# A memset on GpSimd behind every indirect gather of a deformable convolution

## The chip, the core and the metric

The kernel runs on one core of a Trainium2 chip. The metric is device microseconds (us) for one execution of the whole program; a kernel's time is the median over several runs. A profiled execution is a separate run with the hardware profiler on, and it is longer than the plain ones, so both are given below.

## The reference, cut to what matters

Eight images of 256 channels and 64x64 pixels go through two layers. Each layer group-normalises its input and adds its result to it. Layer 0 is a 3x3 neighbourhood attention with four heads. Layer 1 is a modulated deformable 3x3 convolution: an ordinary 3x3 convolution predicts, for every pixel and each of nine taps, a place to read at and a weight; the four corners round that place are fetched, weighted and summed, and the result is multiplied with the weights of that tap.

```python
x = x + _L0_conv_ref(_gn(x), ...)          # attention
om = conv3x3(_gn(x), w_off) + b_off        # 27 numbers a pixel
py, px = base + tap + om[:18]              # where each of 9 taps reads
v = samp(y0, x0) * ((1 - ly) * (1 - lx)) + samp(y0, x0 + 1) * ((1 - ly) * lx) \
  + samp(y0 + 1, x0) * (ly * (1 - lx)) + samp(y0 + 1, x0 + 1) * (ly * lx)
v = v * sigmoid(om[18:27])
x = x + einsum('bckhw,ock->bohw', v, w)
```

`samp` reads all 256 channels of one pixel, wherever the offset points. That is what the gathers of this case do.

## The kernel before

Work is cut by image (8), by chunk of 8 image rows (8 to an image, 512 pixels each), by tap (9 to a chunk) and by block of 128 pixels (4 to a tap). An image therefore has 72 taps and 288 blocks (`SLOTS`, `BLOCKS`), and the program has 2,304 blocks.

Two streams of work are written out by hand and interleaved under a manual schedule, so each engine runs its instructions in the order in which the code issues them.

The front stream (`fronts`, line 752) does for one image the attention (`attention`, line 555) and then the preparation of layer 1 (`prepare`, line 624): it writes the normalised pixels as rows into a table in DRAM (`to_table`, line 630; each row holds two vertically adjacent pixels, `ts` goes out by SyncE at line 645), predicts the offsets (`offsets`, line 649) and turns them into row indices and corner weights (`positions`, line 668). It also loads the next image (line 91) and takes its statistics on VectorE (line 261).

The sampling stream works on the image before. For each block there are four steps, each in its own function:

- `gather` (line 765): GpSimd issues one indirect DMA (line 771). It fetches for 128 pixels the four corners, 4 KB a pixel, from the table into a buffer `g` of 128 x 1,024 floats. There are ten such buffers (`GATHERS`).
- `scale` (line 779): ScalarE multiplies corner 0 into a sum `s` (line 787).
- `sum_corners` (line 790): VectorE adds corners 1 to 3 with three instructions a block (line 795), two blocks at a time. After the third, the buffer `g` is free.
- `transposes` and `product` (lines 809 and 822): TensorE turns the four sums of a tap (line 816), ScalarE copies them out of PSUM (`vt`, line 819), and TensorE multiplies them with that tap's weights into `po` (line 833). After nine taps `finished` (line 841) adds the residual on VectorE (line 844) and SyncE stores the chunk.

`ahead(i)` (line 799) fixes how far each step runs before the tap that uses it, and the order in which the engines' queues are filled:

```python
scale(i + SCALE_AHEAD)        # 8 blocks ahead, two blocks
scale(i + SCALE_AHEAD + 1)
sum_corners(i + SUM_AHEAD)    # 6 blocks ahead, two blocks
gather(i + LEAD)              # 18 blocks ahead, two blocks
gather(i + LEAD + 1)
```

It is called twice a tap, with a piece of the front stream issued between (line 891). The gather of block i+18 takes the buffer of block i+8. So it waits until VectorE has summed block i+8, which is issued one call of `ahead` later; GpSimd, whose queue holds nothing but gathers after the start, stands at its next gather until a buffer comes free. The last image has no front stream beside it: its 72 taps run alone.

Of the kernel before, what the change touches and what calls it, by code (L numbers as in the profile page):

```python
# [9 lines left out]
F32 = mybir.dt.float32  # L10
# [7 lines left out]
P = 128  # L18
# [30 lines left out]
SUM_AHEAD = 6  # L49
SCALE_AHEAD = SUM_AHEAD + 2  # L50
GATHERS = 10
LEAD = SCALE_AHEAD + GATHERS
STEPS = 2 + 7 * NC + 6 + NC + 1
STEPS_AHEAD = 6
# [3 lines left out]
def preact_kernel(ctx: ExitStack, tc: tile.TileContext, a: dict, out: bass.AP):  # L58
# [17 lines left out]
    nc = tc.nc  # L76
    x = a["x"]
    B = x.shape[0]

    const = ctx.enter_context(tc.tile_pool(name="const", bufs=1))  # L80
# [15 lines left out]
    def const_tile(name, shape):  # L96
        t = const.tile(shape, F32, tag=name, name=name)
        nc.scalar.dma_start(t, a[name])
        return t


    alpha = const_tile("alpha", [P, 1])
    gp = ctx.enter_context(tc.tile_pool(name="gp", bufs=GATHERS))
    w_qkv = [gp.tile([96, 4, C], F32, tag="g", name=f"w_qkv{i}") for i in range(2)]
# [38 lines left out]
    with (  # L143
# [26 lines left out]
        for i in range(min(2, B)):  # L170
# [3 lines left out]
            for o in range(H * WP, ENTRIES, P):  # L174
                n = min(P, ENTRIES - o)
# [585 lines left out]

    rows: dict = {}
    sums: dict = {}

    def gather(i):
        if i >= B * BLOCKS:
            return
        b, n = divmod(i, BLOCKS)
        c, k, j = n // NB // KK, n // NB % KK, n % NB
        g = gp.tile([P, 4 * C], F32, tag="g", name=f"g_{i}")  # L770
        nc.gpsimd.indirect_dma_start(  # L771
            out=g,
            out_offset=None,
            in_=tables[b % 2],
            in_offset=bass.IndirectOffsetOnAxis(ap=found[b, c][0][:, j, k : k + 1], axis=1),
        )
        rows[i] = g

    def scale(i):

        if i >= B * BLOCKS:
            return
        b, n = divmod(i, BLOCKS)
        c, k, j = n // NB // KK, n // NB % KK, n % NB
        s = gp.tile([P, C], F32, tag="s", name=f"s_{i}", bufs=NB + SUM_AHEAD)
        g, w = rows.pop(i), found[b, c][1][:, j, k]
        nc.scalar.activation(s, g[:, 0:C], AF.Copy, scale=w[:, 0:1])  # L787
        sums[i] = s, g, w

    def sum_corners(i):  # L790

        work = [sums[n] for n in (i, i + 1) if n in sums]
        for q in range(1, 4):
            for s, g, w in work:
                nc.vector.scalar_tensor_tensor(  # L795
                    s, g[:, q * C : (q + 1) * C], w[:, q : q + 1], s, ALU.mult, ALU.add
                )

    def ahead(i):

        scale(i + SCALE_AHEAD)
        scale(i + SCALE_AHEAD + 1)
        sum_corners(i + SUM_AHEAD)
        gather(i + LEAD)
        gather(i + LEAD + 1)

# [48 lines left out]
    with tc.manual_schedule(engines=ordered):  # L855
# [4 lines left out]
        while done < STEPS:  # L860
            next(steps, None)
            done += 1
        for i in range(GATHERS):
            gather(i)
        for i in range(0, SUM_AHEAD, 2):
# [5 lines left out]
            sum_corners(i)  # L871
            gather(i + GATHERS)
            gather(i + GATHERS + 1)
        gather(SUM_AHEAD + GATHERS)
        gather(SUM_AHEAD + GATHERS + 1)
# [98 lines left out]
```

## Time and profile before

| what | value |
|---|---|
| median of 3 runs | 5,197.73 us (5,185.96 to 5,206.68) |
| the profiled execution | 5,546.8 us, its span 5,545.0 us |
| mean granted TensorE clock in it | 0.939 |
| busy share: PE, DVE, ACT, POOL | 88%, 75%, 43%, 59% |
| gathers (line 771) | 2,304, mean 1,426 ns on GpSimd |
| moved by the gathers' queue | 1,208 MB, 61.9% of the time of 16 DMA engines |
| sums of corners (line 795) | 6,912, mean 478 ns on VectorE |

PE is TensorE's matmul side, PEld its weight loads, DVE is VectorE, ACT is ScalarE, POOL is GpSimd and SP is SyncE. A row of the table of groups names the line, the engine, the operation, the output and inputs and the count; then its busy time and the mean of one in ns; then the idle time of the engine just before these instructions and what ended most of it. A row of the waits says who waited for whom, then the total us, how often, and the longest. A row of the timeline gives the start in us from the start of the span, the busy us, the engine, the line and the number of instructions merged, and in brackets the idle time before and what ended it. The profiled execution is 6.7% longer than the median of the plain runs.

### The profile page before, as it was taken

The numbers are of one execution on the slowest core, as the hardware profiler recorded it, in microseconds if no ns is written. First come the engines' busy times: TensorE is split into PE (matmuls) and PEld (weight loads), VectorE is DVE, ScalarE is ACT, GpSimd is POOL, SyncE is SP. The second block draws the span as 40 slices with busy tenths as digits, with TensorE's granted clock in tenths as the row PEclk, the third lists the DMA queues.
The fourth block names the chain that finished last, engine by engine and source line by source line (L and its number), as shares of the span: only waits on it lengthen the run. The fifth ranks groups of instructions, "written<-read, shape, count | busy, mean of one in ns | idle before, by whom it ended". The sixth has DMA issues, their size and how long they took to land. (4 is left out here: it accounts for less than half of the span.)

```text
span 5545.0 us, 79699 instructions
## 1 busy us (share of the span) xinstructions
PE 4874.6 (88%) x26592; PEld 2725.8 (49%) x26592; DVE 4170.6 (75%) x10071; ACT 2368.6 (43%) x5184; POOL 3287.5 (59%) x2310
## 2 busy tenths in 40 slices
PE   7979998899988998899988999989898899887677
PEld 4545554455544554455544555445554555443333
DVE  4567787788877787778878787878777777876666
ACT  2334444444444444444444444444444444443333
POOL 0036565666646666566656666566664666647776
PEclk9989999999999999999999999999999999998878
DMA  2067777777787777877787777877778677787777
GB/s 85 21 236 251 247 249 278 262 256 260 262 311 249 266 262 283 289 247 265 260 284 278 252 268 252 302 260 258 252 256 322 242 260 258 274 300 275 274 278 279
DMA packets 476840, 1422.60 MB, mean 257 GB/s; under 512 B 46910, under 2 KB 114750, under 8 KB 476300
## 3 DMA queue, kind: packets, MB, share of 16 engines
q0 software_dynamic: 331776, 1208.11, 61.9%
q1 hardware_dynamic: 141902, 204.27, 10.2%
q10 hardware_dynamic: 2750, 5.12, 0.3%
q8 instruction: 210, 3.44, 0.2%
q14 instruction: 202, 1.65, 0.1%
HBM read 1280.19 MB, written 137.13 MB: 256 GB/s over the span
## 5 line engine op out<-in xcount | busy, mean ns | idle before, releaser
L771 POOL DMA_INDIRECT g<-table,idx x2304 | 3284.9, 1426 | 2236.2 <-DVE s L795 585.5
L795 DVE SCALAR_TENSOR_TENSOR s<-g,wt,s 128x256 f32<-128x256 f32 x6912 | 2796.0, 478 | 566.5 <-ACT s L787 399.9
L833 PE MATMUL po<-vt,w_conv 128*128 128x512 f32 x4608 | 2187.8, 620 | 63.0 <-DVE r L844 37.4
L833 PEld LDWEIGHTS po<-vt,w_conv 128*128 128x128 f32 x4608 | 880.2, 202 | 965.9 <-issue 923.9
L787 ACT ACTIVATE s<-g,wt 128x256 f32<-128x256 f32 x2304 | 1068.5, 509 | 562.5 <-DMA g<-table,idx 464.7
L816 PE MATMUL pt<-ident,s 128*128 128x128 f32 x4608 | 725.0, 295 | 262.7 <-ACT vt L819 129.9
L816 PEld LDWEIGHTS pt<-ident,s 128*128 128x128 f32 x4608 | 547.4, 149 | 557.9 <-issue 184.4
L819 ACT COPY vt<-pt 128x512 f32<-128x512 f32 x1152 | 614.7, 584 | 423.3 <-PE pt L816 271.9
L281 PE MATMUL psq<-xn,w_qkvT 128*128 128x512 f32 x512 | 291.1, 720 | 113.2 <-DVE wk L488 108.4
L359 DVE TENSOR_TENSOR qk<-qk,near_k 128x400 f32<-128x400 f32 x256 | 129.8, 567 | 306.1 <-PE qk L351 165.2
L656 PE MATMUL om<-xn,w_off 128*32 128x512 f32 x2304 | 291.9, 604 | 7.7 <-DVE pos L689 7.4
L289 ACT COPY q<-psq 128x512 f32<-128x512 f32 x128 | 75.0, 586 | 483.7 <-PE psq L281 436.2
L313 PE MATMUL psk<-xn,w_qkvT 128*128 128x264 f32 (+1 forms) x1088 | 249.3, 382 | 10.9 <-ACT k L326 10.9
L313 PE MATMUL psv<-xn,w_qkvT 128*128 128x264 f32 (+1 forms) x1088 | 258.4, 382 | 0.0
L281 PEld LDWEIGHTS psq<-xn,w_qkvT 128*128 128x128 f32 x512 | 112.1, 229 | 290.6 <-DVE wk L488 161.1
L528 ACT COPY acc<-av 128x512 f32<-128x512 f32 x128 | 74.9, 585 | 414.4 <-PE av L521 320.8
L533 PE MATMUL proj<-acc,w_projT 128*128 128x512 f32 x512 | 239.8, 596 | 3.3 <-ACT s L787 2.7
L313 PEld LDWEIGHTS psv<-xn,w_qkvT 128*128 128x128 f32 x1088 | 199.9, 190 | 83.3 <-issue 46.4
L313 PEld LDWEIGHTS psk<-xn,w_qkvT 128*128 128x128 f32 x1088 | 202.3, 191 | 73.3 <-issue 20.2
L351 PE MATMUL qk<-k,q 64*64 64x100 f32 x4096 | 165.3, 260 | 78.5 <-issue 75.4
L351 PEld LDWEIGHTS qk<-k,q 64*64 64x64 f32 x4096 | 119.4, 136 | 155.0 <-issue 139.0
L335 ACT COPY v<-psv 128x320 f32<-128x320 f32 (+1 forms) x272 | 111.5, 417 | 187.3 <-PE psv L313 171.1
(89 smaller groups left out, 3375.0 us busy)
## 6 DMA issues: line engine op xcount, KB each, us to landing
table<-ts SPq DMA_DIRECT2D x384, 176.0 KB
g<-table,idx POOLq DMA_INDIRECT x2304
x<-in_x_dram SPq DMA_DIRECT2D x64, 512.0 KB
x<-x SPq DMA_DIRECT2D x64, 512.0 KB
r<-x SPq DMA_DIRECT2D x64, 512.0 KB
out_dram<-r SPq DMA_DIRECT2D x64, 512.0 KB
w_conv<-in_w_conv_dram ACTq DMA_DIRECT2D x1, 2304.0 KB
w_qkv<-in_w_qkv_dram ACTq DMA_DIRECT2D x2, 384.0 KB
```

Of the source, the lines that this page charges most:

```text
L281: nc.tensor.matmul(ps, w_qkvT[:, ct, m * P : (m + 1) * P], window(self.xn, ct, 4), start=(ct == 0), stop=(ct == NT - 1),)
L313: nc.tensor.matmul(ps[:, : (hi - lo) * WP], w_qkvT[:, ct, o : o + P], self.xn[:, ct, lo:hi, :], start=(ct == 0), stop=(ct == NT - 1),)
L351: nc.tensor.matmul(both[h][64 * t : 64 * t + 64, n : n + NK], self.qt[r, ct, o * T * T : (o + 1) * T * T], kt[r, ct, :, T * o : T * o + KT ...
L359: nc.vector.tensor_mul(qk[:, 2 * jj : 2 * jj + 2, :, h, :], both[h][:, : 4 * NK].rearrange("p (j c k) -> p j c k", j=2, c=NT), near_k.unsq ...
L533: nc.tensor.matmul(ps, w_projT[:, ct, m * P : (m + 1) * P], self.acc[:, ct].rearrange("p (t y x) -> p y t x", y=T, x=T), start=(ct == 0), ...
L656: nc.tensor.matmul(ps[32 * g : 32 * g + 32, :], w_off[:, ct, k, :], window(xn, ct, k), start=(n < 4), stop=(n >= KK * NT - 4),)
L771: nc.gpsimd.indirect_dma_start(out=g, out_offset=None, in_=tables[b % 2], in_offset=bass.IndirectOffsetOnAxis(ap=found[b, c][0][:, j, k : ...
L787: nc.scalar.activation(s, g[:, 0:C], AF.Copy, scale=w[:, 0:1])
L795: nc.vector.scalar_tensor_tensor(s, g[:, q * C : (q + 1) * C], w[:, q : q + 1], s, ALU.mult, ALU.add)
L816: nc.tensor.transpose(pt[ct][:, j, :], s[:, ct * P : (ct + 1) * P], ident)
L819: nc.scalar.copy(v[:, ct, :], pt[ct].rearrange("p b n -> p (b n)"))
L833: nc.tensor.matmul(po[:, m, :], w_conv[:, ct, k, m * P : (m + 1) * P], v[:, ct, :], start=(k == 0 and ct == 0), stop=(k == KK - 1 and ct = ...
```

## The change

Behind each gather GpSimd is given a memset of the first 400 elements (112 in the last image) of a scratch tile `pad` of 128 partitions. Nothing reads `pad`.

```diff
 GATHERS = 10
+
+PACE = 400
+PACE_LAST = 112
 LEAD = SCALE_AHEAD + GATHERS
...
     sums: dict = {}
+    pad = const.tile([P, PACE], F32, name="pad")
 
     def gather(i):
         if i >= B * BLOCKS:
...
             in_offset=bass.IndirectOffsetOnAxis(ap=found[b, c][0][:, j, k : k + 1], axis=1),
         )
         rows[i] = g
+
+        n = PACE if b + 1 < B else PACE_LAST
+        nc.gpsimd.memset(pad[:, :n], 0.0)
```

The built programs differ in GpSimd's queue alone: there, 2,304 memsets stand between the gathers, one behind each. From the third on, a memset waits for the memset before it, since both write `pad`; a gather waits for what it waited for before. The orders of instructions of TensorE, VectorE, ScalarE and SyncE, and what they wait for, are the same.

## The prediction

> **What bounds the kernel now.** I read the page's busy shares first, then stretches of the span, then the waits, then the timeline round single gathers.
>
> ```profile
> PE 4874.6 (88%) x26592; PEld 2725.8 (49%) x26592; DVE 4170.6 (75%) x10071; ACT 2368.6 (43%) x5184; POOL 3287.5 (59%) x2310
> ...
> PEclk9989999999999999999999999999999999998878
> DMA  2067777777787777877787777877778677787777
> ...
> L771 POOL DMA_INDIRECT g<-table,idx x2304 | 3284.9, 1426 | 2236.2 <-DVE s L795 585.5
> ```
>
> TensorE is busy 88% of the span and bounds the first seven images, together with the waits in its in-order neighbours. The last entries of the clock row are lower: the last image is another regime. The table of stretches says how different:
>
> ```profile
> 1000.00:1650.00 650.00, 589.91 (x3305) 332.39 (x3306) 512.42 (x1236) 291.99 (x642) 410.12 (x285) 0.96 0.77 269
> ...
> 4950.00:5545.00 595.00, 424.49 (x1236) 211.50 (x1234) 381.99 (x931) 215.86 (x454) 420.38 (x298) 0.83 0.73 278
> ```
>
> After the length come PE, PEld, DVE, ACT and POOL busy, then clock and DMA share. In the last image PE is busy 71% at a clock of 0.83: nothing is full, so the supply of gathered rows sets the pace. From 346 us (first gather) to 4,950 us seven images take 658 us each, 2.28 us a gather; the last takes 595 us, 2.07 us a gather.
>
> Who waits for the DMA queues, from the waits:
>
> ```profile
> ACT s L787 <- DMA g<-table,idx: 464.7, 263, 9.1
> ...
> ACT ts L642 <- DMA table<-ts: 86.7, 48, 5.5
> ...
> DVE stats L261 <- DMA x<-in_x_dram: 72.7, 22, 9.1
> ```
>
> Of the first row 196 us lie in the last image (same view, from 4,950 us); the other seven have some 38 us each. The next two are transfers that SyncE issues.
>
> What a gather looks like in time, from the timeline of VectorE and GpSimd in the last image:
>
> ```profile
> 5247.06 11.96 DVE L795 SCALAR_TENSOR_TENSOR s<-g,wt,s 128x256 f32<-128x256 f32 x30 [6.94 <-ACT s L787]
> ...
> 5249.86 9.97 POOL L771 DMA_INDIRECT g<-table,idx  x1 [6.44 <-ACT s L787]
> ...
> 5260.14 0.94 POOL L771 DMA_INDIRECT g<-table,idx  x1 [0.30 <-issue]
> 5261.38 0.94 POOL L771 DMA_INDIRECT g<-table,idx  x1 [0.31 <-issue]
> ```
>
> Left alone a gather takes 0.94 us, and the next starts 1.24 us after it. One that starts while VectorE runs sums back to back can be held: here 9.97 us, until 0.81 us after the run of 30 sums is over. Counting the trace's records, 70 of 2,304 gathers take over 5 us, 15 of them in the last image (one every 37 us), and 213 take about 2.84 us. That is where the mean of 1.426 us comes from. Behind a held gather the others follow at 1.24 us, as a run.
>
> **What the Trainium skill says.** "SBUF — State Buffer", section "Who interferes with whom": a VectorE instruction with two SBUF inputs contends with a GpSimd instruction that reads SBUF, not with one that only writes it. The sums read two SBUF tiles and the gather reads its indices, so the 9.97 us above agree; a memset only writes, so it should run beside the sums, which no row of before shows. "GPSIMD Engine Reference", section "Performance versus the Vector engine": a body bound by its port takes 1.03 cycles an element at 1.2 GHz, 0.86 ns. "Perfetto Trace Analysis", section "GPSIMD Engine Instruction": GpSimd durations are unreliable, use the spacing of starts; the trace's two long memsets start 1.14 us apart and are given 1.20 us, so here they nearly agree. "DMA: Bandwidth & Descriptors", section "Issuing engines are not separate DMA queues": all queues run on the same 16 engines and interleave, so gathers and SyncE's transfers compete; the two waits above fit that.
>
> **The change part by part.** Nothing is removed. 2,304 memsets are added to GpSimd's queue, and no other queue is changed.
>
> *Price of a memset.* The nearest row:
>
> ```profile
> L135 POOL MEMSET xn<- 128x1320 f32 x2 | 2.3, 1196 | 0.3 <-POOLq L963 0.3
> ```
>
> The 128x1 memsets of the page's small rows take about 0.10 us, so an element costs (1,196 - 104) / 1,319 = 0.83 ns. 400 elements: 0.10 + 0.33 = 0.43 us; 112: 0.10 + 0.09 = 0.19 us. Sum: 2,016 x 0.43 + 288 x 0.19 = 867 + 55 = 922 us of GpSimd time. Unknown is the gap round it: the 0.30 us between two gathers may swallow part of it (-0.1 us) or a second gap may come (+0.3 us). I take 0, so a run of gathers goes from 1.24 to 1.67 us (1.43 in the last image).
>
> *The added wait.* Each memset waits for the one before it, which ended at least a gather (0.94 us) earlier: nothing. Behind a memset only gathers are queued, and they are waited for by ScalarE's scaling.
>
> *What hides it.* GpSimd's idle time ahead of gathers is 2,236 us: 343 us are the start, 2,304 x 0.30 = 691 us the gap that is always there, so some 1,200 us are true waiting for a buffer, against 922 us. It fits, with 0.12 us a gather to spare. If that cover is gone, a gather's own time becomes the pace (first rival). Part of the time for which gathers are held is cover as well, since the memset should not be held.
>
> *What becomes of a later gather.* A gather is 128 rows of 4 KB, eight for each of 16 DMA engines; the trace's packets take 159 ns at the median and 185 ns on average, 1.27 to 1.48 us a gather. That is slower than 1.24 us: in a run the DMA engines are already behind, and a gather issued 0.43 us later lands only about 1.67 - 1.48 = 0.19 us later. Between landing and scaling lie 5.9 us at the median, and under 2 us for 15 to 18% of the gathers of the first seven images. So the late ones count: some 20 waits of ScalarE an image, each after up to four spaced gathers, 20 x 2 x 0.19 = 8 us an image, 56 us in seven. I let half reach the end: +28 us. Bounds: 0, and +240 us if each of the 140 waits grows by the full 4 x 0.43 us.
>
> *What the spacing frees.* In a run the DMA engines get 0.2 to 0.4 us free behind each gather, and SyncE's packets no longer stand behind several queued gathers. I take half of 86.7 + 72.7 = 159 us off these waits and let half of that reach the end: -40 us (bounds 0 and -159).
>
> *The last image.* Its cycle is: ten buffers come ready together, VectorE sums them in one run, the next gather is held for all of it, the rest goes out at once, PE runs dry and its clock falls. At 1.43 us the gathers go out at the rate at which DMA delivers (1.48), so VectorE meets them two by two (2.4 us of sums in 2.9 us) and leaves gaps in which a gather can start. If a third of the 15 cycles is broken, each falling from 41 us (two holds in the trace, 5,249.86 and 5,290.62) to 20 x 1.48 = 29.6 us: 5 x 11.4 = -57 us. Bounds: +20 us (nothing broken, ten gathers a cycle 0.19 us later, partly hidden) and -169 us (the whole image at 288 x 1.48 = 426 us).
>
> Sum: 28 - 40 - 57 = -69 us, 5,547 - 69 = 5,478 us profiled. The median of the plain runs stands to the profiled execution as 5,197.73 / 5,546.8 = 0.937, so 5,133 us; I say **5,130 us**.
>
> **The rivals.**
>
> *GpSimd becomes the bound: slower.* A gather then costs 1.43 (mean, holds included) + 0.30 + 0.43 = 2.16 us against 2.28 us available, so it decides from a second gap of 0.12 us. With 0.2 us the pace is 2.36 us: 2,016 x 0.08 = +161 us, the last image +10 us, 5,718 profiled, 5,358 plain; with 0.3 us, +363 us, about 5,540. For it: spaced gathers fit fewer to the windows between runs of sums (a run of twelve lasts 4.83 us of a tap's 9.1, so four starts at 1.67 us overrun the 4.3 us left, where four at 1.24 us fit). Against it: many gathers start inside a run unharmed, and a held gather is held less when it starts later. I price it at 5,350 us.
>
> *Hidden: no change.* Most gathers wait for their buffer anyway, and 5.9 us of slack swallow the rest: 5,198 us, within 26 us. The same comes out if the memset spaces nothing, because buffers, not GpSimd, set when gathers go.
>
> *The last image's cycle breaks wholly.* -169 us there and -12 elsewhere: 5,366 profiled, 5,028 plain; with all of the SyncE waits gone too, about 4,930.
>
> **How the numbers follow.** A median of three runs spread over 20 us cannot tell less than about 0.5% (26 us) from no change. Chances: forecast 0.49, the wholly broken cycle 0.07, together 0.56 faster; no change 0.16; GpSimd the bound 0.28. The forecast's own range is 5,060 to 5,170. For eight in ten it must take in no change and the milder half of the slower case: 5,020 to 5,310, which leaves out some 0.05 below and 0.13 above.
>
> **What would show it.** Right: memsets of 0.43 and 0.19 us; starts within a run of gathers 1.67 us apart; ScalarE's wait for gathers no larger than 465 us; fewer than 15 holds over 5 us after 4,950 us and a clock above 0.83 there; the waits for `ts` and `x` down. Wrong: starts at 1.8 us or more with GpSimd's waits for buffers near zero, ScalarE's wait for gathers well above 465 us, and gathers held as often as before; or holds gone while VectorE is held by the memsets, its sums then starting over 0.40 us apart.

## The result, and the profile after

The changed kernel takes **5,286.66 us** (median of four runs, 5,268.08 to 5,302.07) beside 5,202.2 us (5,185.96 to 5,215.46, four runs) for the kernel before beside it: a ratio of 1.0161 [1.0137, 1.0185]. It is 1.6% slower; the forecast was 1.3% faster.

One thing is needed ahead of all numbers. The runs of this study fell on several chips, and these are of two kinds: on some the kernel before takes 5,201 to 5,203 us at the median ("quick chips" below), on others 5,521 to 5,568 us ("slow chips"), and each kept its level from run to run. No chip was used twice, so "chip" stands for the chip and for whatever else lasted through its runs. The ratios of the experiments always compare two kernels on one chip. By the level of the kernel before, the result above is from a quick chip, and the profile of before (5,546.8 us), from which everything was predicted, is from a slow one.

The page of the changed kernel: busy shares, the clock and DMA rows, and the rows of the gather and of the memset.

```profile
PE 4760.0 (90%) x26592; PEld 2650.5 (50%) x26592; DVE 4231.6 (80%) x10071; ACT 2386.1 (45%) x5184; POOL 4129.6 (78%) x4614
...
PEclk9989999999999999999999999999999999999999
DMA  2068777778887877977878778888878787788998
...
L775 POOL DMA_INDIRECT g<-table,idx x2304 | 3158.4, 1371 | 1138.0 <-DVE s L802 373.3
...
L784 POOL MEMSET pad<- 128x400 f32 (+1 forms) x2304 | 973.5, 423 | 1.5
```

GpSimd is busy 78%, and its idle time ahead of gathers has halved. The end of the clock row no longer falls, and the DMA row ends at 9 9 8. At first sight that is the forecast come true: the last image is not starved any more. Stretches of the changed kernel (inside the second image, and the last one), with length, PE, PEld, DVE, ACT and POOL busy, clock, DMA share and GB/s:

```profile
1000.00:1650.00 650.00, 590.87 (x3344) 331.91 (x3342) 530.82 (x1267) 298.29 (x653) 543.62 (x586) 0.97 0.80 275
4845.00:5290.00 445.00, 374.84 (x1165) 176.32 (x1163) 365.09 (x880) 211.19 (x432) 374.51 (x566) 0.93 0.94 356
```

The last image moves 356 GB/s where the page of before had 278. The waits:

```profile
ACT s L794 <- DMA g<-table,idx: 686.2, 549, 8.9
...
ACT ts L645 <- DMA table<-ts: 109.7, 59, 5.6
...
DVE stats L264 <- DMA x<-in_x_dram: 53.9, 14, 7.3
```

ScalarE waits longer and twice as often for gathered rows (page of before: 464.7 us, 263 times). GpSimd's timeline inside an image of the first seven, and in the last:

```profile
2399.25 0.94 POOL L775 DMA_INDIRECT g<-table,idx  x1 [0.16 <-issue]
2400.19 0.45 POOL L784 MEMSET pad<- 128x400 f32 x1
2400.80 0.94 POOL L775 DMA_INDIRECT g<-table,idx  x1 [0.17 <-issue]
...
5003.29 0.20 POOL L784 MEMSET pad<- 128x112 f32 x1
5003.66 1.15 POOL L775 DMA_INDIRECT g<-table,idx  x1 [0.17 <-ACT s L794]
```

The memset starts as the gather ends, and the gap in front of the next gather is 0.16 us in place of 0.30. A run of gathers goes at 1.55 us a gather (before 1.24), and at 1.32 us in the last image.

Compared with the page of before alone, the last image seems to gain a lot: from its first scaling to its last it was 553 us there and is 432 us here, and yet the runs of the changed kernel are slower than those of the kernel before. So the two traces can't be compared with each other, and the first task was to find out why.

### The profile page after: what moved, and what is told of

The parts are those of the page before. It is cut to its first block, busy times and chain, and to the rows that moved or that the text cites. A ratio compares the mean times of both kernels' runs of the same rounds, so it can differ in the third digit from the quotient of the medians.

```text
span 5289.9 us, 82003 instructions
## 1 busy us (share of the span) xinstructions
PE 4760.0 (90%) x26592; PEld 2650.5 (50%) x26592; DVE 4231.6 (80%) x10071; ACT 2386.1 (45%) x5184; POOL 4129.6 (78%) x4614
## 4 chain that ended last, share of the span: by engine, by line
PE 50%; DVE 27%; DMA 13%; POOL 5%; issue 3%; ACT 1%; DVEq 0%; SPq 0%; POOLq 0%; ACTq 0%
PE po L840 19%; DVE s L802 15%; DMA g<-table,idx 9%; PE psq L284 5%; PE pt L823 5%; PE psk L316 4%; POOL g L775 4%; PE psv L316 4%; DMA x<-in_x_dram 3%; PE om L659 2%; PE av L524 2%; PE proj L536 2%; PE gen L389 2%; PE qk L354 2%; DVE x L547 1%
## 5 line engine op out<-in xcount | busy, mean ns | idle before, releaser
L775 POOL DMA_INDIRECT g<-table,idx x2304 | 3158.4, 1371 | 1138.0 <-DVE s L802 373.3
L840 PE MATMUL po<-vt,w_conv 128*128 128x512 f32 x4608 | 2144.8, 610 | 81.6 <-DVE r L851 81.5
L794 ACT ACTIVATE s<-g,wt 128x256 f32<-128x256 f32 x2304 | 1095.2, 509 | 787.3 <-DMA g<-table,idx 686.2
L840 PEld LDWEIGHTS po<-vt,w_conv 128*128 128x128 f32 x4608 | 858.8, 197 | 959.2 <-issue 869.3
L784 POOL MEMSET pad<- 128x400 f32 (+1 forms) x2304 | 973.5, 423 | 1.5
L823 PE MATMUL pt<-ident,s 128*128 128x128 f32 x4608 | 701.3, 285 | 163.8 <-DVE s L802 99.0
L823 PEld LDWEIGHTS pt<-ident,s 128*128 128x128 f32 x4608 | 519.6, 144 | 469.8 <-DVE s L802 130.8
L491 DVE TENSOR_TENSOR wk<-wk,near 100x512 f32<-100x512 f32 x256 | 158.5, 680 | 28.0 <-PE wk L483 28.0
```

What stands on the lines that cost most here:

```text
L491: nc.vector.tensor_mul(wk.rearrange("p (t n) -> p t n", n=T * T), ps[:NK].rearrange("p (t n) -> p t n", n=T * T), near.unsqueeze(1).to_bro ...
L775: nc.gpsimd.indirect_dma_start(out=g, out_offset=None, in_=tables[b % 2], in_offset=bass.IndirectOffsetOnAxis(ap=found[b, c][0][:, j, k : ...
L784: nc.gpsimd.memset(pad[:, :n], 0.0)
L823: nc.tensor.transpose(pt[ct][:, j, :], s[:, ct * P : (ct + 1) * P], ident)
L840: nc.tensor.matmul(po[:, m, :], w_conv[:, ct, k, m * P : (m + 1) * P], v[:, ct, :], start=(k == 0 and ct == 0), stop=(k == KK - 1 and ct = ...
```

## The experiments

The times of all runs, each beside the kernel before on the same chip. "400" and "112" are elements of the memset behind each gather.

| run | first seven images | last image | us | before | ratio [95%] |
|---|---|---|---|---|---|
| the change, recorded | 400 | 112 | 5,286.66 | 5,202.2 | 1.0161 [1.0137, 1.0185] |
| h1_before | none | none | 5,195.38 | 5,200.65 | 0.9998 [0.9982, 1.0013] |
| h2_double | 2 x 400 | 2 x 112 | 5,925.7 | 5,200.65 | 1.139 [1.135, 1.143] |
| h3_four | 4 x 400 behind every 4th | 4 x 112 | 5,368.63 | 5,200.65 | 1.0317 [1.0292, 1.0342] |
| g1_big_before | none, other matmuls | none | 5,389.51 | 5,203.12 | 1.0364 [1.0337, 1.0391] |
| g2_big_first7 | 400, other matmuls | none | 5,466.45 | 5,203.12 | 1.0505 [1.0473, 1.0537] |
| g3_big_after | 400, other matmuls | 112 | 5,490.86 | 5,203.12 | 1.0556 [1.0529, 1.0584] |
| after_again | 400 | 112 | 5,498.88 | 5,567.69 | 0.9869 [0.984, 0.9898] |
| before_again | none | none | 5,572.58 | 5,567.69 | 1.0009 [0.9997, 1.0021] |
| e1_first7 | 400 | none | 5,495.45 | 5,520.65 | 0.9946 [0.9926, 0.9966] |
| f_first7 | 400 | none | 5,529.22 | 5,566.33 | 0.9929 [0.9901, 0.9957] |
| k_first7 | 400 | none | 5,492.78 | 5,527.49 | 0.9941 [0.9917, 0.9966] |
| e2_last | none | 112 | 5,480.59 | 5,520.65 | 0.9918 [0.9893, 0.9942] |
| f_last | none | 112 | 5,532.93 | 5,566.33 | 0.9926 [0.9898, 0.9953] |
| k_last | none | 112 | 5,464.25 | 5,527.49 | 0.9893 [0.9859, 0.9928] |
| k_all112 | 112 | 112 | 5,460.12 | 5,527.49 | 0.9885 [0.9863, 0.9907] |
| e3_tiny | 1 | 1 | 5,531.96 | 5,520.65 | 1.0022 [1.0005, 1.0039] |
| f_before | none | none | 5,579.9 | 5,566.33 | 1.0017 [1.0003, 1.0031] |
| e4_short_before | none | left out | 4,989.72 | 5,520.65 | 0.9028 [0.9005, 0.9051] |

The upper seven are from quick chips, all others from slow ones. The experiments in the order in which they were made:

**One half of the change at a time.** e1_first7, e2_last, and a memset of one element behind every gather, e3_tiny.

```diff
# e1_first7
+        if b + 1 < B:
+            nc.gpsimd.memset(pad[:, :PACE], 0.0)
# e2_last
+        if b + 1 == B:
+            nc.gpsimd.memset(pad[:, :PACE_LAST], 0.0)
# e3_tiny
+        nc.gpsimd.memset(pad[:, :1], 0.0)
```

> The memset of 400 elements in the first seven images alone, none in the last. Theory A (GpSimd close to the bound: a run of gathers goes from 1.24 to 1.55 us a gather, the gathers of the first seven images land later and ScalarE waits for more of them): the whole loss is here, ratio to before 1.014 to 1.020. Theory B (the last image, which is fed at the rate of the gathers, loses when these are spaced): 1.000, within 0.003. Theory C (each memset costs its dispatch, wherever it stands): seven eighths of the loss, 1.014; C is told from A by the kernel with memsets of one element.

> The memset of 112 elements in the last image alone. Theory A: within 0.003 of before, or faster by up to 0.5% if the long holds of the last image occur without the profiler too (the profiled last image went from 595 to some 430 us, which would be 3%; then the plain ratio is 0.97). Theory B: 1.013 to 1.019. Theory C: 1.002.

> A memset of one element behind every gather, so nearly all of the instructions' number and none of their length (0.10 us each instead of 0.45 and 0.21). Theory A: below half of the loss, ratio 1.000 to 1.006. Theory C: the whole loss, 1.014 to 1.018.

Each half alone was faster, 0.9946 and 0.9918, where the recorded whole is slower. None of the theories above had expected a gain in both. The tiny memset changed next to nothing, and in its trace a run still goes at 1.24 us a gather: it fits into the gap that was there, so it tells what a memset costs that delays no gather, on a slow chip. Halves that gain and a whole that loses could mean that they interact, or that this chip was not like the one of the result. The kernel before stood at 5,520.65 us here, beside 5,202.2. The last image in e2_last:

```profile
4960.00:5461.00 501.00, 387.45 (x1167) 189.08 (x1166) 363.43 (x880) 207.93 (x431) 410.49 (x564) 0.87 0.84 315
```

The clock of 0.87 (page of before: 0.83), the DMA share of 0.84 (0.73) and six holds over 5 us in place of 15 are the broken cycle of holds that the prediction described. e1_first7, on this chip and without memsets in its last image, still has 12 holds there and a clock of 0.83, and takes 537 us for it where e2_last takes 486.

**The size of the last image.** e4_short_before leaves out the sampling stream of the last image (its preparation stays).

```diff
-        if i >= B * BLOCKS:
+        if i >= (B - 1) * BLOCKS:
...
-        for n in range(B * SLOTS + 1):
+        for n in range((B - 1) * SLOTS + 1):
```

> The kernel before without layer 1 of the last image: its 288 gathers, scalings, sums, transposes and products and its eight stores are left out. This prices the last image in plain runs. If the plain runs have the cycle of long holds that the profile shows, the time falls by some 560 us to about 4,640 us (ratio 0.892); if they feed it at the rate of the DMA engines (288 x 1.48 us), by some 430 us to about 4,770 us (ratio 0.917). If the profile slows the first seven images as well, its own profiled execution stays above the plain one by 150 us or more.

It took 531 us less (5,520.65 - 4,989.72), close to the 537 us of a last image on this chip (e1_first7). The last image runs alone, and its length adds to the total one for one.

**Both kernels once more, unaltered.** before_again and after_again, on one slow chip.

> The kernel before once more, with its profile, on the chip of this call. Chips have differed: its plain runs took 5,202 us beside the changed kernel and 5,521 us in the first experiments, and its profile (5,547 us) looks like the second. Theory A (the difference lies in the chip, not in the profiler): plain runs and profile agree within 0.5% here, at either level. Theory P (the profiler slows this kernel): the profile is some 6% above the plain runs.

> The changed kernel beside it. If this chip is of the slow kind (before near 5,520 us): the two halves of the change gave 0.9946 and 0.9918 there, so 0.986 if they add up, about 5,445 us; the slower result of the first comparison would then belong to the fast kind of chip alone. If it is of the fast kind (before near 5,200 us): 1.016 again, and the traces of both kernels from one chip show where the 85 us go.

The sign turned round: the whole change gave 0.9869 here. So the halves do not fight each other: on chips where each gains, the whole gains too. These profiled executions also agree with the other runs on their chip (before_again: span 5,583.1 beside a median of 5,572.58; after_again 5,495.4 beside 5,498.88), so nothing here shows a program stretched by its profile. The last image of after_again:

```profile
4985.00:5495.00 510.00, 388.63 (x1160) 192.40 (x1160) 360.84 (x874) 206.65 (x429) 418.91 (x564) 0.85 0.82 309
```

Counting records, the last image fell from 547 us in before_again to 496, and the first seven together from 4,673 to 4,636 us: 51 and 37 of the 88 us between the two spans.

**The halves on another chip, a slow one again.** The same edits, with the kernel before beside them.

> The kernel before with its profile, on the chip of this call. On the two chips of the last experiments it took 5,521 and 5,568 us, beside the recorded result 5,202 us. If this chip is like the last of these, its profile shows what is different there: by the theory of held matmuls (on the slower chips TensorE's runs of small matmuls stop for 1 to 2 us at a time with nothing visible to wait for), the waits of PE and PEld qk by issue fall from over 200 us to near 80 us, and the last image from some 550 us to 430 us. If it is like the slower ones: 1.000 again.

> The memset of 400 elements in the first seven images alone. On a slower chip it gave 0.9946. On a chip where the kernel before takes 5,200 us: theory A (GpSimd close to its bound, later gathers) 1.014 to 1.020, all of the loss; theory B (the loss is in the last image) 1.000.

> The memset of 112 elements in the last image alone. On a slower chip it gave 0.9918. On a chip where the kernel before takes 5,200 us: theory A 0.997 to 1.003, theory B 1.013 to 1.019.

0.9929 and 0.9926: each half gains here too, about as on the first slow chip.

**Is it TensorE's small matmuls?** On slow chips TensorE stops in the attention's 64x64 matmuls with nothing that it waits for. The timeline of TensorE in the kernel before (page of before):

```profile
3003.87 0.93 PE L351 MATMUL qk<-k,q 64*64 64x100 f32 x32
3005.03 0.28 PE L351 MATMUL qk<-k,q 64*64 64x100 f32 x1 [0.23 <-issue]
3005.74 0.24 PE L351 MATMUL qk<-k,q 64*64 64x100 f32 x1 [0.43 <-issue]
3007.13 0.24 PE L351 MATMUL qk<-k,q 64*64 64x100 f32 x1 [1.14 <-issue]
...
3010.64 1.42 PE L351 MATMUL qk<-k,q 64*64 64x100 f32 x25 [0.29 <-issue]
```

Some of these matmuls come one at a time, 0.7 us apart and more, and the 64 of this group take 8.2 us. I replaced the small matmuls by large ones on other operands (the attention's result is another one), without memsets, with those of the first seven images, and with all.

```diff
# g1_big_before, shortened; g2_big_first7 and g3_big_after add the memsets
-                                nc.tensor.matmul(
-                                    both[h][64 * t : 64 * t + 64, n : n + NK],
...
+                for h in range(2):
+                    for ct in range(NT):
+                        nc.tensor.matmul(
+                            both[h][:, : 4 * NK],
+                            w_qkvT[:, ct, h * P : (h + 1) * P],
+                            self.qt[:, ct, : 4 * NK],
...
+                nc.tensor.matmul(
+                    av[:, g, :],
+                    self.vk[:, 0, g * P : (g + 1) * P],
```

> The kernel before with the attention's two groups of small matmuls replaced: per chunk 8 matmuls of 128x400 stand for the 64 of the logits, 4 of 128x256 for the 64 of the weighted sum, with other operands, so the attention's result is another. On the slower chips TensorE stops within these small groups with nothing visible to wait for. Theory S (these stops are what a slower chip costs the first seven images): the time falls by 100 us or more, 0.98 or less. If the stops cost little on the path: within 0.99 to 1.00, as TensorE's busy time for both groups changes by less than 100 us.

> The same with the memset of 400 elements in the first seven images. Theory S (spacing helps the first seven images by making the stops rarer, and costs them through later gathers): without small groups only the cost is left, so it is slower than g1 by 0.5 to 1.6%. If the spacing helps by another way (holds, DMA queue): faster than g1 by 0.5 to 0.8%, as on the unchanged attention (0.9946 and 0.9929).

> The same with both memsets. By the theory of holds in the last image, the second memset gives 40 us here too, whatever the attention is: 0.7% below g2.

The question stayed without an answer. The large matmuls cost more (1.0364, outside both expectations), and these runs fell on a quick chip, where the stops are not found. But they gave the recorded sign back: from g1 to g2 the first seven images' memsets cost 77 us (5,466.45 - 5,389.51), from g2 to g3 the last image's 24 us. And the stand-in without any memset already had a last image in which DMA is full:

```profile
4950.00:5386.00 436.00, 381.57 (x1208) 185.09 (x1208) 376.60 (x911) 217.72 (x449) 321.05 (x294) 0.93 0.96 377
```

**The kernel before on a quick chip, and more memset time.** h1_before is the kernel before, for its trace; h2_double gives two memsets behind each gather; h3_four gives four behind every fourth, the memset time of the change in lumps. (`pad` with 800 elements, for one memset of twice the length, leaves 6.84 KB a partition where the pool `wp` needs 7.91 KB; hence two of 400.)

```diff
# h2_double
+        nc.gpsimd.memset(pad[:, :n], 0.0)
         nc.gpsimd.memset(pad[:, :n], 0.0)
# h3_four
-        nc.gpsimd.memset(pad[:, :n], 0.0)
+        if i % 4 == 3:
+            for _ in range(4):
+                nc.gpsimd.memset(pad[:, :n], 0.0)
```

> The kernel before once more, for its own trace. Theory D (on a faster chip the cycle of holds in the last image is not there): if the chip is of the kind where this kernel takes about 5,200 us, the last 288 gathers take under 450 us, with no more than 5 holds over 5 us, and the small matmuls show no stop over 0.8 us. Rival T (the time before differs for another reason): about 5,200 us with a last image of 530 to 550 us as in the page of before. On a slower chip: about 5,570 us and a last image of 530 to 550 us, which tells nothing new.

> Two memsets behind each gather in place of one (2 x 400 elements, 2 x 112 in the last image): GpSimd's added time doubles to about 1,840 us. Theory G (GpSimd's time makes the gathers late, after a cover of some 1,200 us): the cover is gone and GpSimd bounds the first seven images: 288 gathers at 0.94 + 2 x 0.45 + 0.15 = 2.0 us and 71 us of its other work and the sums' holds make over 690 us an image, so 5,550 to 5,900 us on either kind of chip. Rival P (the pacing is worth more the wider it is): on a slower chip no more than the changed kernel's 5,500 us.

> Four memsets behind every fourth gather in place of one behind each: the same GpSimd time, without even spacing. Theory G (GpSimd's time decides): as the changed kernel, 1.5% above before on a faster chip. Rival E (the even spacing decides): the gain of 1.3% is lost on a slower chip (0.995 or more), or the loss on a faster chip differs from the changed kernel's by over 0.5%.

These runs fell on a quick chip, and h1_before settles the question of the two traces: a profiled execution takes 5,195.58 us here, among the other runs (5,189.94 to 5,218.56). Stretches of the kernel before there:

```profile
1000.00:1650.00 650.00, 600.64 (x3448) 337.89 (x3447) 536.26 (x1296) 304.99 (x672) 425.55 (x298) 0.97 0.80 282
4770.00:5194.00 424.00, 369.94 (x1168) 177.16 (x1167) 364.15 (x881) 209.28 (x432) 317.11 (x282) 0.93 0.96 374
```

The last image takes 410 us with no memset at all (553 in the page of before). DMA is busy 96% at 374 GB/s: it is all but full, so there is next to nothing that spacing could free. Seven holds over 5 us remain of the 15 (two more than expected), with DMA busy through them. Among the weight loads of the same kernel's small `qk` matmuls no stop over 0.8 us is left (48 such stops, 57 us, in the trace of before). Its rows of the waits:

```profile
POOL g L771 <- DVE s L795: 615.7, 414, 13.6
...
ACT s L787 <- DMA g<-table,idx: 513.1, 434, 8.9
...
ACT ts L642 <- DMA table<-ts: 120.3, 64, 5.5
...
DVE stats L261 <- DMA x<-in_x_dram: 82.1, 23, 9.3
```

This is the right partner of the profile after, though it may be from another quick chip. Per image (from first scaling to first scaling, in the last to its last scaling), h1_before and the changed kernel have 656.7, 631.3, 628.6, 630.2, 628.9, 630.3, 619.4 and, last, 410.2 us, against 673.2, 639.1, 636.9, 638.6, 636.8, 641.3, 632.8 and 432.2: 73 us more in the first seven, 22 us more in the last, 95 of the 96 us between the spans (5,289.9 - 5,193.8).

What the delay does is read from h2 and h3. The waits of GpSimd and ScalarE in h2_double:

```profile
POOL g L775 <- issue: 523.5, 1478, 10.9
...
POOL g L775 <- DVE s L803: 4.5, 7, 0.6
```
```profile
ACT s L795 <- DMA g<-table,idx: 2079.5, 1396, 8.7
```

GpSimd waits 4.5 us for VectorE to free a buffer, where the kernel before waits 615.7: with 2.17 us a gather in a run it has become the bound, and ScalarE waits 2,080 us for it. That is the slower rival, at twice the dose, and a little beyond the 5,900 us expected. (The 71 us of other work an image, in the expectation, stand in no trace: after the start GpSimd runs gathers and memsets alone.) The lumps of h3_four in GpSimd's timeline:

```profile
2406.65 0.94 POOL L775 DMA_INDIRECT g<-table,idx  x1 [0.30 <-issue]
2407.89 0.95 POOL L775 DMA_INDIRECT g<-table,idx  x1 [0.30 <-DVE s L804]
2409.15 0.94 POOL L775 DMA_INDIRECT g<-table,idx  x1 [0.30 <-issue]
2410.40 0.94 POOL L775 DMA_INDIRECT g<-table,idx  x1 [0.30 <-ACT k L329]
2411.33 1.92 POOL L786 MEMSET pad<- 128x400 f32 x4
2413.54 0.94 POOL L775 DMA_INDIRECT g<-table,idx  x1 [0.30 <-ACT s L796]
```

Four gathers go in 6.89 us. In the order h1_before, changed kernel, h3_four, h2_double, four gathers of a run take 4.96, 6.2, 6.89 and 8.7 us, and ScalarE's wait for gathers is 513, 686, 997 and 2,080 us; the spans grow by 96, 178 and 727 us over h1_before. The changed kernel and h3_four clear the same elements (973.5 and 937.5 us of memset time), but h3_four loses nearly twice as much (178 against 96 us). So it isn't the memsets' own time that costs, but what they add to a run of gathers. Evenly laid, a memset runs partly in the 0.30 us gap that is there anyway; a lump adds its whole 1.92 us, and the gap behind it stays 0.30. In the first seven images the loss goes with the time so added: four gathers of a run take 1.24 us more in the changed kernel and 1.93 us more in h3_four, and these images take 73 and 113 us more. An effect of the lumps as such, beside this, is not shown.

**The halves and a shorter memset once more.**

```diff
# k_all112 (k_first7 and k_last are e1_first7 and e2_last again)
-PACE = 400
+PACE = 112
```

> The memset of 400 elements behind the gathers of the first seven images only. Theory L (on a faster chip later gathers alone count): +73 us, 1.014. On a slower chip 0.993 to 0.995, as twice before.

> The memset of 112 elements behind the gathers of the last image only. Theory L: +22 us on a faster chip, 1.004; my prediction's step (the cycle of holds breaks) would give a gain of up to 57 us, 0.99. On a slower chip 0.992, as twice before.

> 112 elements behind every gather of all images. A run of gathers then goes at 1.32 us in place of 1.55. Theory L (cost in proportion to the delay within a run, 0.08 us against 0.31): first seven images +19 us, the last +22 us, 1.008 on a faster chip. Rival B (a memset inside the gap costs nothing in the first seven images): 1.004. On a slower chip: 0.992 if only the last image gains, 0.987 if the short memset paces the first seven as well.

These runs fell on a slow chip: 0.9941, 0.9893 and 0.9885. The gain of each half is there a third time. With 112 elements throughout, the kernel is as fast as with them in the last image alone, the intervals overlapping: in the first seven images the short memset gains nothing that can be measured, where 400 elements gain. The shorter memset wasn't tried on a quick chip.

## Why the prediction was wrong

The forecast was 5,130 us, 1.3% faster; measured were 5,286.66 us, 1.6% slower. The time lies in the range given (5,020 to 5,310), in the part that the slower rival brought into it; that speaks for no step of the forecast.

**The step that failed first** is the last of the sum: "The median of the plain runs stands to the profiled execution as 5,197.73 / 5,546.8 = 0.937". I took that ratio for a property of profiling that scales every stage alike, and the text ahead of the prediction calls a profiled execution longer than the plain ones. The runs show that it takes as long as the others on its chip. The 6.7% was the distance between two kinds of chip, and the stages do not scale alike: an image of the first seven takes 3 to 5% less on a quick chip (658.5 to 631.3 us for the second), the last 26% less (553 to 410 us). All terms were priced for a chip on which the result was not measured.

On slow chips the total comes out: 5,130 / 5,197.73 = 0.987, and after_again measured 0.9869 [0.984, 0.9898]. That is partly luck. From before_again to after_again the last image fell by 51 us (forecast 57), which is the step as it was meant. But the first seven fell by 37 us (25 to 37 in the medians of e1_first7, f_first7 and k_first7; forecast 12) though ScalarE's wait for gathers rose from 463.4 to 572.6 us, against a sign that I had named, and though the waits for `ts` and `x`, of which I took half away, stayed as they were (160.0 and 156.5 us together). Something else gained there.

**The last image**, forecast -57 us with +20 us for "nothing broken, ten gathers a cycle 0.19 us later, partly hidden". On a quick chip it cost +22 us between the traces, about that bound. The long holds did fall there, from seven to one, but with DMA busy 0.96 without memsets no starved cycle was left to break; how the 22 us arise was not measured. On slow chips the step is right. It brought -33 to -63 us in e2_last, f_last and k_last. Beside the run on the same chip that has memsets in the first seven images alone, their last images took 486, 498 and 473 us in place of 537, 527 and 525, with 6, 8 and 5 holds in place of 12, 12 and 14, and the clock there was 0.87 to 0.89 in place of 0.83 to 0.84.

**A later gather**, forecast +28 us. On a quick chip the first seven images grew by 73 us, net of what the spacing frees. Here a term was mis-sized, and one reason is in how it was built: I let the 20 waits of an image that were there grow by 0.38 us each. ScalarE's wait for gathers up to the end of the seventh image, in h1_before and in the changed kernel:

```profile
ACT s L787 <- DMA g<-table,idx: 328.8, 223, 8.9
```
```profile
ACT s L794 <- DMA g<-table,idx: 489.3, 340, 8.9
```

The figures are the total us, the number of waits and the longest. The mean wait stays at 1.4 to 1.5 us; there are 117 more of them. Gathers that had landed just in time now land late. In the first seven images 19% of the gathers of h1_before land less than 2 us before they are scaled, and 29% of those of the changed kernel. The slack itself was smaller than I had read it: from landing to scaling the median is 5.9 us in the slow trace of before, 4.3 us in h1_before and 2.9 us in the changed kernel. The half that I let through was near: 73 of the 160 us added reach the end, net of the other terms.

**What the spacing frees**, forecast -40 us. The two waits fell by 10.6 (`ts`, 120.3 to 109.7) and 28.2 us (`x`, 82.1 to 53.9), 39 of the 80 us that I took off them. If half reached the end, as I assumed, it gave -19 us; that half was not measured by itself.

**The price of a memset**, 0.43 and 0.19 us: measured 0.45 and 0.21 us, 973.5 us in all for 922. The gap, taken at 0, shrank by 0.14 us, a little beyond the bound of -0.1 us that I gave. The Trainium skill, "SBUF — State Buffer", section "Who interferes with whom", holds for the memset: it only writes, and in the changed kernel's trace the 928 long memsets that ran beside a sum took 448 ns on average, the 1,088 others 457, while the sums keep their 476 ns (before 478).

**The cover**, 1,200 us of true waiting. It was counted rightly for the slow trace; by the same working h1_before has some 960 us (1,987.0 less 336 at the start and 691 of gaps). It was also judged wrongly. GpSimd still waits 373.3 us for VectorE's sums after the change, so it has not become the bound, and the first rival's pace of 2.36 us a gather did not come about. But idle time in sum says nothing on whether a gather of a run has time: the waits lie ahead of runs, and the memsets lie inside them. (A slip in the third rival, on which nothing rests: its terms give about 4,917 us, not 4,930.)

**What stays open.** First, what makes a chip slow, and what the first seven images gain there. The gathers' own 0.94 us, the 159 ns of the median DMA packet and the gap of 0.30 us are the same on both kinds. What differs is that on slow chips TensorE stops with no visible releaser ("issue"). The trace of before:

```profile
PE qk L351 <- issue: 75.4, 132, 1.7
...
PE po L833 <- issue: 25.6, 9, 3.9
PE pt L816 <- issue: 16.8, 25, 4.2
```

No trace from a quick chip has such a row for TensorE's matmuls. The stops in `qk` lie in the first seven images, 30.8 of the 42.4 us of those in `po` and `pt` in the last. With memsets of 400 elements in the first seven images, on slow chips, the `qk` stops of over 0.8 us vanish (48 in the trace of before, none in e1_first7, f_first7, k_first7 and after_again), but short ones come up in `av`, the other group of small matmuls (1.5 us in the trace of before):

```profile
PE av L524 <- issue: 38.2, 112, 0.6
```

That row is of after_again. k_all112 keeps 29 of the long `qk` stops, 34 us, and its short memsets gained nothing measurable in the first seven images. So the stops may be what 400 elements take away there; it is not shown, since the experiment meant to remove them fell on a quick chip. Image lengths of single traces can't decide it: on one slow chip the same code took 4,612 us for the first seven images in e2_last and 4,658 in e4_short_before. Second, the halves of the change on the unaltered kernel were not run on a quick chip; the split of 73 and 22 us is from the image lengths of two traces, and g1 to g3 agree with 77 and 24 us.

## What to carry to other kernels

When a profiled execution lies outside the spread of the plain runs, it doesn't describe them: don't scale it, but ask what differs, and price each step for both cases; a gain that depends on a starved stage (a clock of 0.83, DMA at 0.73) is the first that may be missing. A delay in a prefetch is not priced by the waits that exist, but by how many transfers land just in time: count those with less slack than the delay, since each becomes a new wait. Work put into an in-order queue costs by what it adds to a run, gaps included, not by its own length or by its sum against the queue's idle time.

## What the runs showed of the hardware

- Two kinds of chips, 6 to 7% apart in this program: 5,201 to 5,203 us (three chips or sets of runs), and 5,521 to 5,568 us (four). Such a group of 64 small matmuls, 8.2 us in the slow chip's trace above, goes in one piece on a quick one, in h1_before's timeline:

```profile
2892.28 1.63 PE L351 MATMUL qk<-k,q 64*64 64x100 f32 x64
```

- A memset of 128 x 400 elements between two gathers costs 0.31 us, not 0.45: the 0.30 us ahead of the next gather shrinks to 0.16. Two in a row (h2_double) show a gather's gap of 0.30 us again in the trace's run at 2.17 us.
- A memset of one element behind each gather is nearly free on a slow chip, 1.0022 [1.0005, 1.0039]; its own 0.12 us disappear in the gap.
- Of the 1,113 gathers that were held over 5 us in all traces, 1,099 end 0.80 to 0.84 us after VectorE's last sum, with memsets or without. In 628 of them VectorE had by then gone on to the residual adds (`r`, line 844), which read PSUM and one SBUF tile: the gather is let go although VectorE is busy.
